# RWKV attention with routed experts: the experts' activations transposed by DMA in 16-bit halves, and their down products a step later

## The chip, the cores and the metric

The kernel runs on one core of a Trainium2 chip. The metric is the device time of one execution in microseconds (us). TensorE (PE, with its weight loads as PEld) multiplies matrices into PSUM, VectorE (DVE), ScalarE (ACT) and GpSimd (POOL) work on elements, SyncE (SP) issues most DMAs; GpSimd issues the gathers, the scatters and the accumulating DMAs. Each engine has one queue and works through it in order; a DMA that is issued runs by itself.

## The reference

On 2048 tokens of 512 channels, all in float32, with `xn = layernorm(x)`:

```
r, v, k = split(xn @ W_rvk.T)                      # attention branch
y = sigmoid(r) * wkv(time_decay, time_first, k, v) # a recurrence over 8 x 256 = 2048 tokens
                                                   # (the input is 1 x 2048 x 512)
attn = y @ W_out.T

probs = softmax(xn @ classifier_w.T)               # 12 choices: 8 experts, 4 without weights
idx = top_k(probs + bias, 2); rw = probs[idx] * 1.5
expert_e = (silu(xn @ gate_e.T) * (xn @ up_e.T)) @ down_e.T     # inner size 256
ffn = sum_e w_e * expert_e + xn * (weight of the 4 without weights)

out = x + attn + ffn
```

## The kernel before

**The beginning.** `x` is normalised, stored as `xs` in DRAM, and transposed into `xnT`; the router finds for each token its two experts, and lays out 25 tiles of 128 places, each of one expert (`token_i`: which token stands at a place, `to_i`: which row of `out` it is added to, `wplace`: with which weight). `out` is filled with `x` by DMA (`begin_output`). Every later part is added to `out` by accumulating DMAs, except for the last block of 512 tokens, which is read back (`read_out`), added up on VectorE and written. The accumulating DMAs on `out` follow one another, each waiting for the earlier one that may touch the same rows; a scatter may touch all of them.

**The middle** is a list of work written out by hand: `table` holds entries with a due time and is sorted by it. The due times are no times of the machine; they set the order only, and each engine's queue has the instructions in that order. There are three kinds:

- `project(b, c)` for block `b` and channel group `c`: three groups of matmuls (`pk`, `pv`, `pr`), each of four matmuls of 128x512 (eight records, since each is done in two passes), evicted from PSUM by ScalarE. Two PSUM banks (`ps_mm`) serve them in turn. Eight entries of `attention` (output products `pw`, four matmuls each) take places among them (`after`).
- `scan(*unit)`: the recurrence of one block and channel group in four stages: scan 0 (VectorE), exponentials (ScalarE), two scans and five elementwise operations (VectorE), reciprocal and product `yT` (VectorE). Scan 0 is 2.7 us, the third stage about 5.3, the last about 4.
- `step(i, n)`: one step of the experts' pipeline over the 25 tiles. A tile is gathered (`gather`, GpSimd), packed into 16-bit halves by ScalarE and transposed by a DMA of SyncE (`flip`: `xp`, then `xq`), united to float32 by ScalarE (`unite`: `xgT`), multiplied with the expert's gate and up weights (`up`: `pg`, four matmuls), put through `silu(g) * u` (`activate`: `th` on ScalarE and VectorE, `act` on VectorE), transposed by TensorE through PSUM (`turn_act`: two transposes into `pa`, and `actT` by ScalarE), multiplied with the down weights (`finish`: `po`, two matmuls of 128x512), weighted (`yo`, ScalarE) and scatter-added to `out` (GpSimd). In step `i` the gate and up products of tile `i` are made, with the transposes of tile `i - 1`'s activations in their middle and its down products behind them. Weights are loaded two steps ahead (`fetch`, `fetch_down`), with three buffers each.

**The end.** After the table come the last tile's transposes, the output products of block 2 (`last_rows`, with the last tile's down products after the first of them), a conditional loop for more than 25 tiles which is not entered, and block 3: reading back, its output products, the last sums and the writing of them. The order of that last part, after `manual.close()`, is no longer set by hand.

Pools give the number of buffers: `ex_p` two of each tag, `wk1` one, `gathered` two, `rows` three, `ewp` three.

Of the kernel before, what the change touches and what calls it, by code (L numbers as in the profile page):

```python
# [26 lines left out]
F32 = mybir.dt.float32  # L27
BF16 = mybir.dt.bfloat16
I32 = mybir.dt.int32
U16 = mybir.dt.uint16  # L30
# [5 lines left out]
P = 128  # L36
T = 2048
C = 512
# [7 lines left out]
INTER = 256  # L46
IC = INTER // P
# [4 lines left out]
TILES = 25  # L52
# [7 lines left out]
def layer(ctx: ExitStack, tc: tile.TileContext, x, w_rvk, w_out, decay, first, cls, ebias, gu, down, out):  # L60
    nc = tc.nc

    def pool(name, bufs, **kw):
        return ctx.enter_context(tc.tile_pool(name=name, bufs=bufs, **kw))
# [6 lines left out]
    wk1 = pool("wk1", 1)  # L71
# [6 lines left out]
    ex_p = pool("exp", 2)  # L78
# [180 lines left out]
    def project(b, c):  # L259

        n = f"{b}_{c}"
        for name, m in (("k", 2), ("v", 1), ("r", 0)):
            ps = ps_mm.tile([P, TB], F32, tag="mm", name=f"p{name}{n}")
            for k in range(CC):
                nc.tensor.matmul(  # L265
                    ps,
                    wrvk_sb[m][:, k, c * P : (c + 1) * P],
                    xnT[b][:, k, :],
                    start=(k == 0),
                    stop=(k == CC - 1),  # L270
                )
                if k < CC - 1:
                    yield
            t = kvp.tile([P, TB], F32, tag=name, name=f"{name}{n}")
            if name == "r":
                nc.scalar.activation(t, ps, AF.Exp, scale=-1.0)
            else:
                nc.scalar.copy(t, ps)
            kvr[b, c, name] = t
            yield  # L280
# [270 lines left out]
    st = {}  # L551

    def gather(i, token=token_i):

        xg = gathered.tile([P, C], F32, tag="xg", name=f"xg{i}")
        nc.gpsimd.indirect_dma_start(  # L556
            out=xg,
            out_offset=None,
            in_=xs,
            in_offset=bass.IndirectOffsetOnAxis(ap=token[:, i : i + 1], axis=0),  # L560
        )
        st[i] = {"xg": xg}

    def fetch(i, which=which_i):

        e = nc.values_load(
            which[0:1, i : i + 1],
            engines=(SP,),
            min_val=0,
            max_val=E - 1,  # L570
            skip_runtime_bounds_check_because="a sum of E - 1 comparisons",
        )
        w = ewp.tile([P, CC, 2 * INTER], F32, tag="gw", name=f"gw{i}")
        nc.sync.dma_start(w, gu[bass.ds(e, 1)].rearrange("o p c n -> p (o c) n"))
        st[i].update(w=w, e=e)

    def fetch_down(i):
        d = ewp.tile([P, IC, C], F32, tag="dw", name=f"dw{i}")
        nc.sync.dma_start(d, down[bass.ds(st[i]["e"], 1)].rearrange("o p c n -> p (o c) n"))
        st[i]["d"] = d  # L580
# [9 lines left out]

    def flip(i):

        xp = ex_p.tile([P, 2, C], U16, tag="xp", name=f"xp{i}")
        nc.scalar.copy(xp, st[i]["xg"].bitcast(U16).rearrange("p (c h) -> p h c", h=2))  # L594
        xq = ex_p.tile([P, 2 * CC, P], U16, tag="xq", name=f"xq{i}")
        nc.sync.dma_start_transpose(xq, xp.rearrange("p h c -> p (h c)"))
        st[i]["xq"] = xq

    def unite(i):

        xgT = ex_p.tile([P, CC, P], F32, tag="xgT", name=f"xgT{i}")
        nc.scalar.copy(  # L602
            xgT.bitcast(U16).rearrange("p c (t h) -> p c t h", h=2),
            st[i]["xq"].rearrange("p (h c) t -> p c t h", h=2),
        )
        st[i]["xgT"] = xgT

    def up(i, cs):

        if 0 in cs:  # L610
            st[i]["pg"] = ps_gu.tile([P, 2, INTER], F32, tag="gu", name=f"pg{i}")
        pg = st[i]["pg"]
        for c in cs:
            nc.tensor.matmul(  # L614
                pg, st[i]["xgT"][:, c, :], st[i]["w"][:, c, :], start=(c == 0), stop=(c == CC - 1)
            )

    def activate(i):
        pg = st[i]["pg"]

        th = ex_p.tile([P, INTER], F32, tag="th", name=f"th{i}")
        nc.scalar.activation(th, pg[:, 0, :], AF.Tanh, scale=0.5)  # L622
        nc.vector.scalar_tensor_tensor(th, th, 1.0, pg[:, 0, :], ALU.add, ALU.mult)  # L623
        act = ex_p.tile([P, INTER], F32, tag="act", name=f"act{i}")
        nc.vector.tensor_mul(act, th, pg[:, 1, :])
        st[i]["act"] = act

    def turn_act(i):
        pt = ps_tr.tile([P, IC, P], F32, tag="tr", name=f"pa{i}")
        for c in range(IC):  # L630
            nc.tensor.transpose(pt[:, c, :], st[i]["act"][:, c * P : (c + 1) * P], ident)  # L631
        actT = ex_p.tile([P, IC, P], F32, tag="actT", name=f"actT{i}")
        nc.scalar.copy(actT, pt)  # L633
        st[i]["actT"] = actT

    def finish(i, weight=wplace, to=to_i):
        po = ps_o.tile([P, C], F32, tag="o", name=f"po{i}")
        for c in range(IC):
            nc.tensor.matmul(  # L639
                po, st[i]["actT"][:, c, :], st[i]["d"][:, c, :], start=(c == 0), stop=(c == IC - 1)  # L640
            )
        yo = rows.tile([P, C], F32, tag="rb", name=f"yo{i}")
        nc.scalar.activation(yo, po, AF.Identity, scale=weight[:, i : i + 1])  # L643
        nc.gpsimd.indirect_dma_start(  # L644
            out=out,
            out_offset=bass.IndirectOffsetOnAxis(ap=to[:, i : i + 1], axis=0),
            in_=yo,
            in_offset=None,
            compute_op=ALU.add,
        )  # L650
        del st[i]

    def step(i, n):

        if i + 2 < n:
            fetch(i + 2)
        if i < n:
            up(i, (0, 1))
        if i > 0:
            turn_act(i - 1)  # L660
        if i < n:
            up(i, (2, 3))
            activate(i)
        if i + 3 < n:
            gather(i + 3)
        if i > 0:
            finish(i - 1)
        if i + 2 < n:
            flip(i + 2)
            fetch_down(i + 2)  # L670
        if i + 1 < n:
            unite(i + 1)

# [61 lines left out]
    fill(4)  # L735
    next(stages[0])
    flip(0)
    flip(1)
    fill(4)
    next(stages[0])  # L740
# [5 lines left out]

    UNIT = 20.0
    ahead = [p for p in [project(*u) for u in units[LEAD:]] for _ in range(3)]  # L750
    after = {14: (0, 0), 17: (0, 1), 20: (0, 2), 23: (0, 3), 34: (1, 0), 37: (1, 1), 40: (1, 2), 43: (1, 3)}
    groups = len(ahead) + len(after)
    total = groups * 3.43 + TILES * 5.5
    table = []
    for u in range(1, len(units)):
        for k, at in enumerate((0, 4, 6, 12)):
            table.append(((u - 1) * UNIT + at, 1, stages[u]))
    for m in range(groups):
# [7 lines left out]
    for i in range(TILES):  # L766
        table.append((6 + total * i / TILES, 1, iter([(step, i, TILES)])))
# [9 lines left out]
    last_rows = attention(NTB - 2)  # L777
    next(last_rows)
    finish(TILES - 1)
    read_xn(NTB - 1)  # L780
    whole(last_rows)
# [9 lines left out]
    with tc.If(count > TILES):  # L791
        with tc.For_i(TILES, MAX_TILES, 1) as i:
            cols = {}
            for name, a, dt in (
                ("which", which_i, I32), ("token", token_i, I32), ("to", to_i, I32), ("weight", wplace, F32)
            ):
                cols[name] = small.tile([P, 1], dt, tag=f"col_{name}", name=f"col_{name}")
                nc.vector.tensor_copy(cols[name], a[:, bass.ds(i, 1)])
            gather(0, cols["token"])
            fetch(0, cols["which"])  # L800
            fetch_down(0)
            turn(0)
            up(0, range(CC))
            activate(0)
            turn_act(0)
            finish(0, cols["weight"], cols["to"])
# [46 lines left out]
```

## Time and profile before

| what | value |
|---|---|
| median of 3 runs | 397.49 us (396.98 to 397.56) |
| the profiled execution | 398.03 us |
| its span | 396.2 us |
| DMA, mean | 216 GB/s, 85.78 MB |
| DMA transposes `xq` | 25, issue 1.25 us each on SyncE, landing 2.8 / 4.8 / 5.1 us (min / median / max) |
| scatters to `out` | 25, landing 4.9 / 5.6 / 10.1 us |
| rows added to `out` (L722) | 12, landing 4.0 / 5.3 / 6.7 us |
| `xp` copy, `xgT` copy, `actT` copy (ScalarE) | 1.04, 1.16, 0.37 us |
| SyncE's waits before `xq` | 212.4 us in 24 waits, for ScalarE |

The profile lists instructions by line of the kernel, engine and operation with the names of the tiles (`pg<-gw,xgT` writes `pg` from `gw` and `xgT`). Times are in us from the span's start. In the order of time, a line gives start, duration, engine, line, operation, and in brackets how long the engine was idle before it and what ended that. A matmul's end is modelled: of consecutive matmuls, the distance of their starts says what one costs.

### The profile page before, as it was taken

How to read it: one execution, taken by the hardware profiler on the slowest of the kernel's cores; microseconds unless marked ns; L12 is line 12 of the kernel's file. 1: busy time of each engine (PE TensorE's matmuls, PEld its weight loads, DVE VectorE, ACT ScalarE, POOL GpSimd, SP SyncE). 2: the span in 40 equal slices, each digit the busy share in tenths (PEclk: the TensorE clock that was granted, in tenths of full speed). 3: DMA queues.
4: the chain of work that ended last, by engine and by line, in shares of the span. 5: the costliest groups of instructions: out<-in, count | busy, mean ns of one | idle time of the engine just before them, and what ended most of it. 6: DMA issues, size and time to landing. Idle time of an engine off the chain costs nothing. (4 is left out here: it accounts for less than half of the span.)

```text
span 396.2 us, 3539 instructions
## 1 busy us (share of the span) xinstructions
PE 379.4 (96%) x1040; PEld 173.8 (44%) x1040; DVE 271.1 (68%) x397; ACT 154.0 (39%) x255; POOL 98.5 (25%) x130
## 2 busy tenths in 40 slices
PE   0999999999999999999999999999999999999996
PEld 0555445444444444444444444444444444444442
DVE  4872998997673919766659395569395784883905
ACT  2765111553444453344354443354444253432000
POOL 4002001420232414133333232222142331122220
PEclk9999999999999999999999999999999999999999
DMA  7998907645765855879778899765857979664593
GB/s 270 409 393 315 318 28 321 142 148 185 240 191 145 261 158 201 256 230 282 215 170 226 239 242 257 220 187 141 282 191 231 266 220 278 151 119 91 124 169 149
DMA packets 50372, 85.78 MB, mean 216 GB/s; under 512 B 29680, under 2 KB 29808, under 8 KB 46576
## 3 DMA queue, kind: packets, MB, share of 16 engines
q1 hardware_dynamic: 42816, 64.84, 48.0%
q0 software_dynamic: 7536, 20.71, 25.2%
q8 instruction: 8, 0.13, 0.1%
q14 instruction: 12, 0.10, 0.1%
HBM read 63.78 MB, written 19.40 MB: 210 GB/s over the span
## 5 line engine op out<-in xcount | busy, mean ns | idle before, releaser
L614 PE MATMUL pg<-gw,xgT 128*128 128x512 f32 x200 | 93.9, 592 | 0.0
L644 POOL DMA_INDIRECT out_dram<-yo,to_i x25 | 42.4, 1697 | 147.3 <-ACT yo L643 116.6
L265 PE MATMUL pk<-xnT,wrvk 128*128 128x512 f32 x128 | 58.8, 596 | 0.0
L265 PE MATMUL pr<-xnT,wrvk 128*128 128x512 f32 x128 | 57.7, 592 | 0.0
L265 PE MATMUL pv<-xnT,wrvk 128*128 128x512 f32 x128 | 57.6, 593 | 0.0
L707 PE MATMUL pw<-wout_sb,yT 128*128 128x512 f32 x128 | 56.8, 593 | 0.1
L323 DVE RECIPROCAL den<-den 128x512 f32<-128x512 f32 x16 | 53.5, 3345 | 0.0
L614 PEld LDWEIGHTS pg<-gw,xgT 128*128 128x128 f32 x200 | 36.1, 190 | 36.3 <-issue 34.9
L639 PE MATMUL po<-dw,actT 128*128 128x512 f32 x100 | 47.1, 593 | 0.5 <-ACT actT L633 0.5
L309 DVE TENSOR_TENSOR_SCAN sums<-obv,state,a 128x512 f32<-128x512 f32 x16 | 20.5, 1283 | 35.0 <-ACT obv L303 35.0
L623 DVE SCALAR_TENSOR_TENSOR th<-th,pg 128x256 f32<-128x256 f32 x25 | 10.5, 419 | 41.8 <-ACT th L622 41.7
L556 POOL DMA_INDIRECT xg<-xs,token_i x25 | 29.8, 1193 | 33.1 <-DVE empty L543 27.5
L707 PEld LDWEIGHTS pw<-wout_sb,yT 128*128 128x128 f32 x128 | 24.2, 190 | 30.6 <-issue 30.6
L265 PEld LDWEIGHTS pk<-xnT,wrvk 128*128 128x128 f32 x128 | 23.8, 190 | 31.2 <-issue 31.2
L265 PEld LDWEIGHTS pr<-xnT,wrvk 128*128 128x128 f32 x128 | 24.2, 190 | 30.1 <-issue 30.1
L265 PEld LDWEIGHTS pv<-xnT,wrvk 128*128 128x128 f32 x128 | 24.2, 190 | 30.1 <-issue 29.9
L643 ACT ACTIVATE yo<-po,wplace 128x512 f32<-128x512 f32 x25 | 17.2, 687 | 35.9 <-PE po L639 35.9
L639 PEld LDWEIGHTS po<-dw,actT 128*128 128x128 f32 x100 | 18.9, 190 | 24.7 <-issue 23.4
L602 ACT COPY xgT<-xq 128x1024 uint16<-128x1024 uint16 x25 | 29.0, 1160 | 0.0
L594 ACT COPY xp<-xg 128x1024 uint16<-128x1024 uint16 x25 | 25.8, 1037 | 0.0
L633 ACT COPY actT<-pa 128x256 f32<-128x256 f32 x25 | 9.3, 371 | 37.8 <-PE pa L631 37.8
L230 PE MATMUL pt<-ident,x 128*128 128x128 f32 x64 | 12.6, 326 | 11.8 <-DVE x L220 10.1
(149 smaller groups left out, 360.3 us busy)
## 6 DMA issues: line engine op xcount, KB each, us to landing
gw<-in_gu_dram SPq DMA_DIRECT2D x25, 1024.0 KB, 6.9
dw<-in_down_dram SPq DMA_DIRECT2D x25, 512.0 KB, 5.3
x<-in_x_dram SPq DMA_DIRECT2D x16, 256.0 KB, 5.3
xs<-x SPq DMA_DIRECT2D x16, 256.0 KB, 4.7
wrvk<-in_w_rvk_dram SPq DMA_DIRECT2D x3, 1024.0 KB, 7.3
xrow<-xs SPq DMA_DIRECT2D x12, 256.0 KB, 5.7
out_dram<-xrow POOLq DMA_DIRECT2D x12, 256.0 KB, 5.3
wout_sb<-in_w_out_dram SPq DMA_DIRECT2D x1, 1024.0 KB, 9.5
```

The costliest lines, as they stand in the source:

```text
L230: nc.tensor.transpose(pt[:, j * P : (j + 1) * P], xt[b * NJ + j][:, c * P : (c + 1) * P], ident)
L265: nc.tensor.matmul(ps, wrvk_sb[m][:, k, c * P : (c + 1) * P], xnT[b][:, k, :], start=(k == 0), stop=(k == CC - 1),)
L309: nc.vector.tensor_tensor_scan(sq, bs, a2, s[:, 3:4], ALU.add, ALU.mult)
L323: nc.vector.reciprocal(den, den)
L556: nc.gpsimd.indirect_dma_start(out=xg, out_offset=None, in_=xs, in_offset=bass.IndirectOffsetOnAxis(ap=token[:, i : i + 1], axis=0),)
L594: nc.scalar.copy(xp, st[i]["xg"].bitcast(U16).rearrange("p (c h) -> p h c", h=2))
L602: nc.scalar.copy(xgT.bitcast(U16).rearrange("p c (t h) -> p c t h", h=2), st[i]["xq"].rearrange("p (h c) t -> p c t h", h=2),)
L614: nc.tensor.matmul(pg, st[i]["xgT"][:, c, :], st[i]["w"][:, c, :], start=(c == 0), stop=(c == CC - 1))
L639: nc.tensor.matmul(po, st[i]["actT"][:, c, :], st[i]["d"][:, c, :], start=(c == 0), stop=(c == IC - 1))
L643: nc.scalar.activation(yo, po, AF.Identity, scale=weight[:, i : i + 1])
L644: nc.gpsimd.indirect_dma_start(out=out, out_offset=bass.IndirectOffsetOnAxis(ap=to[:, i : i + 1], axis=0), in_=yo, in_offset=None, compute ...
L707: nc.tensor.matmul(po, yT[b][:, c, j * P : (j + 1) * P], wout_sb[:, c, :], start=(c == 0), stop=(c == CC - 1),)
```

## The change

The activations of 23 of the 25 tiles go through ScalarE and a DMA transpose, as the gathered tokens do: `flip_act` packs `act` into halves (`ap`) and SyncE transposes them (`aq`), and `unite_act` makes `actT` of them one step later. The down products of tile `i - 2` are made in step `i` where those of `i - 1` were. The last two tiles keep the transposes on TensorE, and the last step has two tiles' down products. The down weights are fetched one step later. `xp` gets one buffer in place of two. The due times are set a little closer (19.4 for 20.0 a unit of the scan, 280.92 for 288.42 in all).

```diff
     def flip(i):
 
-        xp = ex_p.tile([P, 2, C], U16, tag="xp", name=f"xp{i}")
+        xp = wk1.tile([P, 2, C], U16, tag="xp", name=f"xp{i}")
...
+    def flip_act(i):
+
+        ap = wk1.tile([P, 2, INTER], U16, tag="ap", name=f"ap{i}")
+        nc.scalar.copy(ap, st[i]["act"].bitcast(U16).rearrange("p (c h) -> p h c", h=2))
+        aq = wk1.tile([P, 2 * IC, P], U16, tag="aq", name=f"aq{i}")
+        nc.sync.dma_start_transpose(aq, ap.rearrange("p h c -> p (h c)"))
+        st[i]["aq"] = aq
+
+    def unite_act(i):
+        actT = ex_p.tile([P, IC, P], F32, tag="actT", name=f"actT{i}")
+        nc.scalar.copy(
+            actT.bitcast(U16).rearrange("p c (t h) -> p c t h", h=2),
+            st[i]["aq"].rearrange("p (h c) t -> p c t h", h=2),
+        )
         st[i]["actT"] = actT
...
         if i + 2 < n:
             fetch(i + 2)
-        if i < n:
-            up(i, (0, 1))
-        if i > 0:
+        if i > 1:
+            unite_act(i - 2)
+        if 0 < i < n - 1:
+            flip_act(i - 1)
+        up(i, (0, 1))
+        if i == n - 1:
             turn_act(i - 1)
-        if i < n:
-            up(i, (2, 3))
-            activate(i)
+        up(i, (2, 3))
+        activate(i)
         if i + 3 < n:
             gather(i + 3)
-        if i > 0:
+        if i > 1:
+            finish(i - 2)
+        if i == n - 1:
             finish(i - 1)
         if i + 2 < n:
             flip(i + 2)
-            fetch_down(i + 2)
+        if 2 <= i + 1 < n:
+            fetch_down(i + 1)
         if i + 1 < n:
             unite(i + 1)
...
-    UNIT = 20.0
+    UNIT = 19.4
...
-    total = groups * 3.43 + TILES * 5.5
+    total = groups * 3.43 + TILES * 5.2
```

More of the change, by code (lines that the diff above doesn't have):

```diff
@@ L634, in turn_act @@
         st[i]["actT"] = actT
+    def flip_act(i):
[10 more added lines that the diff above has]
+        )
+        st[i]["actT"] = actT
     def finish(i, weight=wplace, to=to_i):
```

## The prediction

> **What bounds the kernel now.** I read four views, in this order: the page, the table by stage, the order of time in one expert step, and the order of time at the end.
>
> ```profile
> PE 379.4 (96%) x1040; PEld 173.8 (44%) x1040; DVE 271.1 (68%) x397; ACT 154.0 (39%) x255; POOL 98.5 (25%) x130
> PEclk9999999999999999999999999999999999999999
> ```
>
> TensorE is busy for 96% of the span at the full clock. The table by stage says where the other 4% lies (columns: stretch, length, busy time of each engine, clock, DMA share, GB/s):
>
> ```profile
> 110.00:140.00 30.00, 29.55 (x73) 12.99 (x72) 19.27 (x22) 13.33 (x22) 10.49 (x8) 1.00 0.72 214
> 170.00:200.00 30.00, 30.00 (x75) 13.43 (x74) 21.24 (x24) 11.36 (x20) 10.73 (x10) 1.00 0.92 257
> 370.00:396.20 26.20, 22.19 (x52) 9.32 (x50) 11.62 (x14) 0.00 (x0) 5.15 (x5) 1.00 0.59 130
> ```
>
> In the expert steps TensorE never stops, except for 0.45 us in one of them (step 4: its down products waited for `actT`, behind a state copy on ScalarE that waited for VectorE). Any TensorE instruction taken out there shortens the stretch. The order of time in step 9 gives the price of one tile's transposes and ScalarE's room:
>
> ```profile
> 180.32 3.60 PE L265 MATMUL pk<-xnT,wrvk 128*128 128x512 f32 x8
> 183.75 1.88 PE L614 MATMUL pg<-gw,xgT 128*128 128x512 f32 x4
> 183.95 0.58 ACT L278 COPY k<-pk 128x512 f32<-128x512 f32 x1 [1.80 <-PE pk L265]
> 185.47 0.38 PE L631 MATMUL pa<-ident,act 128*128 128x128 f32 x2
> 185.68 1.88 PE L614 MATMUL pg<-gw,xgT 128*128 128x512 f32 x4
> 185.94 0.37 ACT L633 COPY actT<-pa 128x256 f32<-128x256 f32 x1 [1.41 <-PE pa L631]
> 187.40 1.88 PE L639 MATMUL po<-dw,actT 128*128 128x512 f32 x4
> 187.60 0.38 ACT L622 ACTIVATE th<-pg 128x256 f32<-128x256 f32 x1 [1.29 <-PE pg L614]
> ```
>
> Eight matmuls of 512 columns take 183.75 - 180.32 = 3.43 us. The same eight with the two transposes between take 187.40 - 183.75 = 3.65 us. So a pair costs 0.22 us, and not the 0.38 of its row, which overlaps its neighbours.
>
> The end is another matter. GpSimd's rows there:
>
> ```profile
> 358.26 0.92 POOL L722 DMA_DIRECT2D out_dram<-xrow  x1 [5.07 <-DVE xrow L719]
> 363.55 1.61 POOL L644 DMA_INDIRECT out_dram<-yo,to_i  x1 [4.37 <-ACT yo L643]
> 370.15 1.56 POOL L644 DMA_INDIRECT out_dram<-yo,to_i  x1 [5.00 <-DMA out_dram<-yo,to_i]
> 375.59 2.73 POOL L722 DMA_DIRECT2D out_dram<-xrow  x3 [3.88 <-DVE xrow L719]
> 379.30 0.86 POOL L722 DMA_DIRECT2D out_dram<-xrow  x1 [0.97 <-DVE xrow L719]
> ```
>
> The adds into `out` go one after another: the last scatter (370.15) waited for the one before it to land, and the rows at 375.59 for the last scatter (the first of those rows was ready on VectorE at 374.21, over a microsecond earlier). Then the reading back of the last block starts at 382.29, VectorE gets it at 386.23, and its last add starts at 392.38, when TensorE is done. There this chain is only 1.50 us ahead of TensorE.
>
> **What the change removes.** 23 of the 25 pairs of transposes (the last two tiles keep theirs): 23 x 0.22 = 5.1 us of TensorE on the path. The down products come a step later with `actT` long ready, so step 4's 0.45 us goes too: 5.5 us. The profiled run took 398.03 us with a span of 396.2; the sum is made on the span and taken off the median 397.49, 0.54 us under that run.
>
> **What it adds, and what hides it.** ScalarE: the packing of 512 halves (new). The rows nearest are 1.04 us for 1024 halves and 0.58 to 0.63 us for 512 elements: 0.52 to 0.63. The uniting: half of 1.16, or 0.63. Less the 0.37 us of `actT`, this is 0.7 to 0.9 us a tile, about 18 us in 154. It stands ahead of `th`, where ScalarE is empty from 184.53 to 187.60 less 0.37, or 2.7 us, in most steps (1.6 in two, none in step 4). If that cover is gone, `th` is late by up to 1.3 us, and TensorE notices only if an eviction of `pk`, `pv` or `pr` behind it comes after both banks are full. I take 0.
>
> ScalarE's new waits: packing waits for VectorE's `act`. Behind it on ScalarE stand `th`, `yo` and the evictions. In all 24 steps `act` was ready 2.9 to 8.9 us before ScalarE came there; 0. Uniting waits for a transfer issued a step earlier. Steps start 12.2 us apart, a few 8.8; from the issue to the next uniting 7.4 us is left in a short step. The transfer's landing isn't shown; the `xq` transfer of twice the size lands in 2.8 to 5.1 us, and a lower bound is the 1.25 us that SyncE spends on issuing one. I take the upper end, as it queues behind the 1 MB of `gw`; 0. The skill's page "DMA: Bandwidth & Descriptors" (section "Anatomy of one DMA") has about 2.0 us plus bytes over 436 GB/s for a GpSimd transfer; for 128 KB that is an estimate of 2.3 us, and the sum would be the same.
>
> SyncE: each step issues one more transpose (1.25 us), ahead of `xq` and `dw`. It spent 212 us waiting at `xq` for ScalarE; 0. DMA: 23 x 128 KB is 3 MB more on 85.8; shares reach 0.92 in some stages, yet loads have two steps of lead; 0.
>
> A rule speaks against all this. "VectorE: DVE Perf Modes" (section "Rules for kernel authors") sends a 128x128 transpose to TensorE wherever PSUM will do as its goal. By that rule nothing is won and the time stays at 397.49. The stage's row says otherwise of this kernel: there TensorE has no idle time, and ScalarE and SyncE have.
>
> `xp` with one buffer: in the steps its last reader lands a step earlier; 0. In the beginning flips 0 and 1 follow each other, and the second copy must wait for the first transfer: issued at 73.15, landed 2.8 to 5.1 us later, then 1.05 us of copy and 0.58 of evicting `v`: 77.6 to 79.9. TensorE needs that bank at 78.26. I take 2.8, since DMA is idle before 75 (share 0.21): no stall; the other end is 1.6 us.
>
> `dw` is fetched one step later for products two steps later: its lead grows from one step to two. In step 23 SyncE now has this load and a transpose ahead of the last rows' loads, which ran from 341.75 to 362.47 and are needed by VectorE after 366; 0. Timetable: sorted by its new due times (total 280.9 for 288.4, units 19.4 for 20.0), the order stays but for nine pairs of neighbours. Three put ScalarE's exponentials ahead of work it would have done first (two evictions, the last step); there ScalarE may wait for VectorE's 2.7 us of scan 0, which is due 4 us before; 0. The last scan ends earlier, so VectorE's rows at the end wait for TensorE alone.
>
> **What the change moves to the end.** Step 24 now has two down products. TensorE comes to them 5.5 us earlier plus the 1.72 us of the product that step 1 no longer has: 7.2 us. So scatter 22 takes the place of 363.55 at 356.3. Scatter 23 is ready 1.7 us later but must wait for 22 to land; scatter 24 for 23; the rows for 24. Before, only one such wait stood between there and the rows. Its price, issue to next issue: 6.60 (363.55 to 370.15), 5.44 (370.15 to 375.59), in the steps 6.1 to 7.3 where a row waited for a scatter. I take 6.6 (loads beside it, as before), 6.2 (middle of the rows), 5.4: 356.3 + 18.2 = 374.5, only 1.1 us before 375.59. Four rows at 0.91 (2.73 / 3): 378.2, against 380.16 before (379.30 + 0.86). Reading back starts 2.13 us on (380.16 to 382.29), VectorE 3.94 on (to 386.23), at 384.3. Its eight operations (386.23 to 390.88, and one of 0.69) take 5.3: 389.6, against 393.07. So the end comes 3.5 us earlier, and TensorE, ending at 386.9, waits for it. 397.49 - 3.5 = **394.0 us**. Bounds: three gaps of 5.44 give the full 5.5; three of 7.33 give 378.3 for the first row, and an end at 393.3, 0.2 us later than now.
>
> **Rivals.** *The full gain*: the chain at the end keeps up and TensorE's 5.5 us arrive whole, 392.0 us. For it: the two last gaps were short, with few loads beside. Against: all three gaps must be as short as the shortest that the trace has, 5.44 us.
>
> *Slower through the scatters at the end*: the same three gaps, longer. From 7.24 us each on, nothing is left; at 8.0 the end is 2.3 us later, 399.8 us. For it: one landing took 10.1 us. Against: the median is 5.6 and load falls in the end.
>
> *ScalarE waits after all*: for the transfer, or in the beginning (1.6 us); half of the gain goes: 397.49 - 1.75 = 395.7 us, within the range.
>
> *It does not do what it says*: if weight loads rather than matmuls set the pace, the pair would not cost 0.22; the 3.65 against 3.43 excludes it.
>
> **How the numbers follow.** Chain at the end as worked out: 0.60; full gain 0.14; ScalarE or the beginning 0.12; scatters at the end at no gain or slower 0.14. A measurement of this kernel tells about 0.2%, 0.8 us, from no change. Faster: 0.60, 0.14 and 0.08 of the third, 0.82; same: 0.04 of the third and 0.03 of the last, 0.07; slower: the rest of the last, 0.11. The range reaches from the full gain, 392.0, to 396.6, which leaves out the worst gaps.
>
> **What would show it.** Two `pa` groups in place of 25, TensorE busy about 5 us less and still full in the steps; scatters of the end about 6 us apart with DMA as releaser; VectorE's last adds waiting for the reading back and not for `pw`. Wrong, if TensorE shows gaps in the steps with `xgT` or evictions as releaser, or if its last product again ends last.

## The result, and the profile after

The changed kernel takes 399.72 us (median of four runs, 398.75 to 399.91), the kernel before beside it 397.34 us: 1.0056 of the time before, interval 1.0038 to 1.0074. It is 0.6% slower, where 394.0 us had been predicted. Runs more than 1.5% above the fastest of their kernel are left out of medians and ratios; this concerns three of twelve runs of one version below, with the rows of block 1 earlier. The profiled execution took 399.70 us with a span of 397.9 us, 1.67 us more than the one of before.

The page first, its lines of busy time and of the clock:

```profile
PE 374.3 (94%) x994; PEld 169.8 (43%) x994; DVE 270.6 (68%) x397; ACT 170.7 (43%) x278; POOL 99.0 (25%) x130
PEclk9999999999999999999999999999999999999997
```

TensorE has 5.1 us less to do (379.4 before), ScalarE 16.7 us more. The last digit of the clock is 7 where TensorE idles at the end. The table by stage (stretch, length, busy time of each engine, clock, DMA share, GB/s):

```profile
110.00:140.00 30.00, 29.02 (x68) 12.65 (x67) 17.27 (x22) 14.00 (x25) 8.96 (x8) 1.00 0.87 240
170.00:200.00 30.00, 30.00 (x71) 13.27 (x70) 21.28 (x25) 14.26 (x24) 10.66 (x9) 1.00 1.05 267
370.00:397.90 27.90, 17.80 (x41) 7.33 (x39) 6.62 (x10) 0.00 (x0) 5.16 (x5) 0.92 0.59 132
```

The steps are still full, but the stretch from 110 us now lacks 0.98 us of TensorE where it had lacked 0.45. In the last stretch TensorE works 17.8 of 27.9 us: it no longer sets the end. One step in order of time shows the new pipeline at work:

```profile
180.95 3.60 PE L614 MATMUL pg<-gw,xgT 128*128 128x512 f32 x8
181.82 0.68 ACT L646 COPY actT<-aq 128x512 uint16<-128x512 uint16 x1
182.40 0.62 ACT L639 COPY ap<-act 128x512 uint16<-128x512 uint16 x1
184.39 1.88 PE L655 MATMUL po<-dw,actT 128*128 128x512 f32 x4
184.59 0.38 ACT L622 ACTIVATE th<-pg 128x256 f32<-128x256 f32 x1 [1.57 <-PE pg L614]
```

The eight gate/up matmuls take 184.39 - 180.95 = 3.44 us, with no transposes in their middle (3.65 before). The two copies stand in ScalarE's idle time, and `th` still waits for TensorE. So the mechanism works where it was meant to. GpSimd's rows at the end show what took the gain:

```profile
353.88 0.92 POOL L743 DMA_DIRECT2D out_dram<-xrow  x1 [4.88 <-issue]
358.90 1.67 POOL L660 DMA_INDIRECT out_dram<-yo,to_i  x1 [4.10 <-ACT yo L659]
368.39 1.56 POOL L660 DMA_INDIRECT out_dram<-yo,to_i  x1 [7.83 <-issue]
374.12 1.55 POOL L660 DMA_INDIRECT out_dram<-yo,to_i  x1 [4.17 <-issue]
379.44 3.61 POOL L743 DMA_DIRECT2D out_dram<-xrow  x4 [3.77 <-DMA out_dram<-yo,to_i]
```

Three scatters (22, 23 and 24) in a row, and then the four rows at once. All of them were ready before: scatter 22's `yo` at 357.16, scatter 23's at 358.88, the first row's sum on VectorE at 365.83, the last one's at 374.61. The rows begin at 379.44, where those of before began at 375.59. The chain of waits now ends in this list and no longer in TensorE:

```profile
354.72 3.45 PE po L655 x8
358.90 24.65 DMA out_dram<-yo,to_i
383.68 5.17 DMA orows<-out_dram
```

And VectorE waits for the reading back, not for `pw`. Its last add before the change (L716), and its last rows after it:

```profile
392.38 0.69 DVE L716 TENSOR_TENSOR orows<-orows,pw 128x512 f32<-128x512 f32 x1 [1.50 <-PE pw L707]
```

```profile
388.87 2.08 DVE L715 SCALAR_TENSOR_TENSOR orows<-xrows,zw,orows 128x512 f32<-128x512 f32 x3 [14.26 <-DMA orows<-out_dram]
392.12 1.87 DVE L737 TENSOR_TENSOR orows<-orows,pw 128x512 f32<-128x512 f32 x3
```

TensorE's end moved from 392.35 to 387.95 us, 4.4 us earlier; VectorE's last add ends at 394.0, 0.9 us later than before.

**Where the list becomes full.** All 37 adds into `out` (25 scatters and 12 rows) follow one another. In the kernel before, the last eight intervals between them, from the row at 324.17 to the first of the last rows at 375.59, had room left: four of the adds (339.44, 351.57, 358.26 and 363.55) were issued within 0.7 us of their source. In the changed kernel the same stretch runs from the row at 319.68 to 379.44 and has nine intervals, since the lag (the down products two steps behind, for one) leaves one tile more to be added there. Every one of these adds came 1.7 us or more after its source, once the one before had landed: 59.76 / 9 = 6.64 us each. The lag brings one add of 6.6 us more to an end that had about 1.5 us of room, and TensorE's 4.4 us do not cover it.

### The profile page after: what moved, and what is told of

It reads as the page before. It is cut to its first block, busy times and chain, and to the rows that moved or that the text cites. A ratio compares the mean times of both kernels' runs of the same rounds, so it can differ in the third digit from the quotient of the medians.

```text
span 397.9 us, 3507 instructions
## 1 busy us (share of the span) xinstructions
PE 374.3 (94%) x994; PEld 169.8 (43%) x994; DVE 270.6 (68%) x397; ACT 170.7 (43%) x278; POOL 99.0 (25%) x130
## 4 chain that ended last, share of the span: by engine, by line
PE 76%; DMA 9%; DVE 7%; ACT 4%; issue 2%; DVEq 0%; SPq 0%; ACTq 0%
PE pg L614 21%; PE pr L265 12%; PE pk L265 12%; PE pv L265 11%; PE po L655 10%; PE pw L728 7%; DMA out_dram<-yo,to_i 6%; PE pt L230 2%; DMA orows<-out_dram 1%; DMA x<-in_x_dram 1%; ACT x L222 1%; DVE tok L512 1%; PE pi L520 1%; ACT xnT L231 0%; DVE orows L715 0%
## 5 line engine op out<-in xcount | busy, mean ns | idle before, releaser
L614 PE MATMUL pg<-gw,xgT 128*128 128x512 f32 x200 | 90.1, 592 | 0.0
L614 PEld LDWEIGHTS pg<-gw,xgT 128*128 128x128 f32 x200 | 37.9, 190 | 47.4 <-issue 46.2
L556 POOL DMA_INDIRECT xg<-xs,token_i x25 | 30.6, 1224 | 42.9 <-DVE empty L543 27.5
L309 DVE TENSOR_TENSOR_SCAN sums<-obv,state,a 128x512 f32<-128x512 f32 x16 | 20.5, 1282 | 25.3 <-ACT obv L303 25.3
L655 PEld LDWEIGHTS po<-dw,actT 128*128 128x128 f32 x100 | 18.9, 190 | 25.2 <-issue 23.2
L622 ACT ACTIVATE th<-pg 128x256 f32<-128x256 f32 x25 | 9.6, 383 | 42.8 <-PE pg L614 42.8
## 6 DMA issues: line engine op xcount, KB each, us to landing
wout_sb<-in_w_out_dram SPq DMA_DIRECT2D x1, 1024.0 KB, 10.1
```

The costliest lines, as they stand in the source:

```text
L309: nc.vector.tensor_tensor_scan(sq, bs, a2, s[:, 3:4], ALU.add, ALU.mult)
L556: nc.gpsimd.indirect_dma_start(out=xg, out_offset=None, in_=xs, in_offset=bass.IndirectOffsetOnAxis(ap=token[:, i : i + 1], axis=0),)
L614: nc.tensor.matmul(pg, st[i]["xgT"][:, c, :], st[i]["w"][:, c, :], start=(c == 0), stop=(c == CC - 1))
L655: nc.tensor.matmul(po, st[i]["actT"][:, c, :], st[i]["d"][:, c, :], start=(c == 0), stop=(c == IC - 1))
```

## The experiments

Theory A: the two scatters of the last step, one add more in a serial list, decide the time; TensorE's gain is real. Against it stood: the DMA transposes themselves (their packets beside the scatters) make the landings long; the place of five loads that start there does; the denser timetable does. In each paragraph the ratio is to the kernel before on the same chip.

**Control.** The changed kernel again, beside three of the runs below (catching up in step 17, the loads, the old timetable). The others ran at other times, some on another chip; the kernel before took 397.66 to 397.77 us beside all of them.

> The changed kernel again, beside the next ones: 399 to 400 us by every theory.

398.76 us (12 runs, 396.86 to 400.88), 1.0027, interval 1.0008 to 1.0045. A kernel whose end is this list scatters by 4 us from run to run here; the kernel before stayed within 2.0 us in the 29 runs beside it (396.63 to 398.62). Differences below 1 us between two kernels of the first sort mean little. Its profile has the first of the last rows at 376.96 and a span of 396.1.

**One add fewer at the end.** Tile 22's scatter goes to another tensor in DRAM.

```diff
+    aside = dram.tile([T + P, C], F32, tag="aside", name="aside")
...
-            out=out,
+            out=aside if i == TILES - 3 else out,
```

> The changed kernel, but tile 22's scatter goes to another DRAM tensor (its share is left out of the output), so that nothing that adds into out follows it any more. Theory A (the chain of adds into out at the end sets the time, and the second scatter of the last step is a link too many): scatter 23 goes out near 359 in place of 368.4, the four rows near 372 in place of 379.4, and TensorE ends last again; 393 to 394.5 us. Rival B (every DMA has become slower through the 23 more transposes, and the one link is of little account): 397 to 399. Rival C (the loss lies in the steps, not at the end): 399.7, unchanged.

394.08 us, 0.9920, interval 0.9905 to 0.9935. GpSimd's rows at the end:

```profile
356.53 1.87 POOL L661 DMA_INDIRECT aside<-yo,to_i  x1 [3.35 <-DMA out_dram<-xrow]
358.70 1.62 POOL L661 DMA_INDIRECT out_dram<-yo,to_i  x1 [0.30 <-issue]
367.50 1.55 POOL L661 DMA_INDIRECT out_dram<-yo,to_i  x1 [7.17 <-issue]
372.90 3.62 POOL L744 DMA_DIRECT2D out_dram<-xrow  x4 [3.85 <-DMA out_dram<-yo,to_i]
```

Scatter 23 takes the place that scatter 22 had. The rows come 6.5 us earlier than at 379.44, and 4.1 us earlier than the control's; the median falls by 4.7 us against the control. All of the new DMA load is still there. One serial add fewer turns a loss of 0.3 to 0.6% into a gain of 0.8%.

**The lag alone.** The kernel before with the down products two steps behind, TensorE's transposes and the old due times.

```diff
-        if i > 0:
+        if i > 1:
+            finish(i - 2)
+        if i == n - 1:
             finish(i - 1)
...
-            fetch_down(i + 2)
+        if 2 <= i + 1 < n:
+            fetch_down(i + 1)
```

> The kernel before with one part of the change: down products two steps behind and down weights fetched a step later, with TensorE's transposes kept and the old due times. Theory A: TensorE's work is that of before, but the last step's two scatters put one gap of some 6 us into the chain at the end; about 1 us slower than before, 398 to 399 us. Rival B (the transposes by DMA are what slows): no change, 397.3.

400.61 us, 1.0069, interval 1.0056 to 1.0082: more than was expected of it, and slower than the whole change. Its end:

```profile
360.79 1.61 POOL L644 DMA_INDIRECT out_dram<-yo,to_i  x1 [4.19 <-ACT yo L643]
369.50 1.56 POOL L644 DMA_INDIRECT out_dram<-yo,to_i  x1 [7.11 <-issue]
375.05 1.55 POOL L644 DMA_INDIRECT out_dram<-yo,to_i  x1 [3.99 <-issue]
380.48 3.62 POOL L723 DMA_DIRECT2D out_dram<-xrow  x4 [3.88 <-DMA out_dram<-yo,to_i]
```

Not one activation is transposed by DMA here, and the three intervals are 8.71 + 5.55 + 5.43 = 19.7 us, as in the control (8.61 + 5.66 + 5.22 = 19.5). The first row is 4.9 us later than before; less the 1.5 us that the list was ahead of TensorE, this is 3.4 us, and the span grew by 3.5 (399.7 for 396.2). Up to there this list had room: scatters 20, 21 and 22 and the row at 355.68 came within 0.5 us of their sources. So the last step's additional scatter makes the loss without a list that is full from 319 us on. The lag costs about 3 us by itself; the transposes by DMA then win part of it back through an earlier start (358.90 or 357.47 for 360.79).

**Catching up earlier.** The lag of two ends in step 17, which makes two tiles' down products; from there on TensorE transposes and the products follow one step behind. The last step then has one tile's products, as before.

```diff
-        if i > 1:
+        if 1 < i <= 17:
             unite_act(i - 2)
-        if 0 < i < n - 1:
+        if 0 < i < 17:
             flip_act(i - 1)
...
-        if i == n - 1:
+        if i >= 17:
             turn_act(i - 1)
...
-        if i > 1:
+        if 1 < i <= 17:
             finish(i - 2)
-        if i == n - 1:
+        if i >= 17:
             finish(i - 1)
```

> The changed kernel up to step 17, which makes two tiles' down products; from there on transposes on TensorE and down products one step behind, as in the kernel before. 17 pairs of transposes are gone: 17 x 0.22 = 3.7 us of TensorE, less the 0.5 us that step 4 now loses. Theory A (the extra link in the chain of the end takes the gain): in the steps around 17 the chain has pauses of several us and swallows the extra scatter, the end is that of the kernel before, and TensorE ends last; 394 to 395 us. Rival B (all DMAs slower through the added transposes): the chain is still full at the end, 397 to 399.

394.55 us (394.00 to 394.62), 0.9914, interval 0.9902 to 0.9927, faster than the kernel before and than the changed one. GpSimd's rows at the end, and the chain that ended last:

```profile
360.12 1.87 POOL L660 DMA_INDIRECT out_dram<-yo,to_i  x1 [4.37 <-ACT actT L633]
368.23 1.56 POOL L660 DMA_INDIRECT out_dram<-yo,to_i  x1 [6.24 <-DMA out_dram<-yo,to_i]
373.60 3.62 POOL L743 DMA_DIRECT2D out_dram<-xrow  x4 [3.80 <-issue]
```

```profile
379.23 9.69 PE pw L728 x22
388.95 0.69 DVE orows L737
```

The additional scatter (tile 16's) was issued 4.2 us late at 281.89, and the next, at 290.13, on time: in the middle the list has room and takes it. At the end TensorE is last again. With 16 pairs removed (the expectation had counted 17), 16 x 0.22 = 3.5 us less the 0.53 us that the stall of step 4 grew by give 3.0; measured 397.68 - 394.55 = 3.1.

**The same, with the uniting earlier.** In step 4 TensorE waits for `actT`. In the changed kernel, ScalarE's rows there and TensorE's wait:

```profile
126.81 0.19 ACT L322 COPY state<-sums 128x2 f32<-128x2 f32 x1 [2.79 <-DVE sums L311]
126.91 0.67 ACT L646 COPY actT<-aq 128x512 uint16<-128x512 uint16 x1
...
127.63 1.98 PE L655 MATMUL po<-dw,actT 128*128 128x512 f32 x4 [0.98 <-ACT actT L646]
```

The uniting stands behind the state copy, which waits for VectorE. Moved to the end of the step before:

```diff
-        if 1 < i <= 17:
-            unite_act(i - 2)
...
         if i + 1 < n:
             unite(i + 1)
+        if 0 < i < 17:
+            unite_act(i - 1)
```

> As the kernel that catches up in step 17, but the uniting of the activations stands at the end of the step in which they were packed, behind the uniting of the next tokens, and not at the beginning of the next step. Theory: the 0.98 us in which TensorE waits in step 4 come from the place of actT behind the state copy on ScalarE; earlier, actT is ready before, TensorE is full from 110 to 140 us (30.00 of 30.00), and since TensorE ends last here, the time is 1 us less than 394.55: about 393.6, 0.990 of the kernel before. Rival: ScalarE now waits in each step for the transfer that was issued in the same step, 5 us in the median, and the yo copy, the evictions of pk, pv and pr and the packing behind it come late: TensorE shows gaps in the steps, the time is 395 or more.

393.55 us (393.06 to 393.73), 0.9893, interval 0.9878 to 0.9908: the fastest version here. By stage, and ScalarE's waits (in total, times, longest):

```profile
110.00:140.00 30.00, 30.00 (x71) 13.30 (x70) 17.68 (x24) 13.81 (x26) 8.39 (x7) 1.00 0.95 245
```

```profile
ACT actT L646 <- DMA aq<-ap: 10.5, 4, 3.6
```

The stall is gone and the time is 1.0 us less, as expected. The rival's wait is there too, 10.5 us in four steps, and no matmul was late for it.

**Catching up in step 22.** As the one in step 17, with the last condition at 22:

```diff
-        if i == n - 1:
+        if i >= 22:
             finish(i - 1)
```

> The changed kernel, but step 22 makes two tiles' down products, and from there on TensorE transposes and the lag is one step; so the last step has one scatter fewer than in the changed kernel, and the additional scatter is issued near 345 us, inside the stretch in which each add into out waited for the one before in the changed kernel (from 319 us on). Theory that counts the whole full stretch: the number of adds from 319 us to the end is the same, only the place of one differs; the chain stays full, the first of the last rows comes at 377 to 379 us, the time 397 to 399.5 us. Theory that counts only the last step: with three adds in place of four behind the last step's products the end has the slack of the kernel before, the first rows come near 374 us and TensorE ends last: 394 to 395 us.

396.36 us, 0.9967, interval 0.9954 to 0.9979: neither theory's time. The list was full from the row at 319.36 on, as the first theory had it, with each add there late by 1.4 us or more, and the first of the last rows came at 375.78, 1.2 us ahead of the control's. The nine intervals took 6.27 us each (56.42 / 9; control 57.33 / 9 = 6.37). The two profiled executions differ by as much, 1.13 us (396.82 and 397.95); the medians differ by 2.4 us because the one profile lies 0.5 us above its median and the other 0.8 us below. A catch-up inside the full stretch thus gives back about half of what one in step 17 does (2.4 us of 4.2 by the medians).

**The loads beside the first scatter of the end.** In the changed kernel scatter 22 takes 8.4 us to land (358.90 to 367.31). The row's landing that releases it also releases five loads of 256 KB on SyncE, issued from 358.20; these are the suspected reason. Here four of the five stand ahead of the row's own and are issued from 344.04.

```diff
+    read_xn(NTB - 1)
...
-    read_xn(NTB - 1)
```

> The changed kernel with the loads of block 3's rows ahead of those of block 2's in SyncE's queue. In the changed kernel the landing of row (1,3) lets go scatter 22 and five loads of 256 KB at the same moment, and the scatter lands after 8.4 us. Theory A2 (those loads make the first gap of the end long): the four loads of block 3 run before, scatter 22 lands after some 6 us, the gap to scatter 23 falls from 9.5 to about 7; 397 to 398 us. Rival (the gap has another reason): unchanged, 399.7.

398.21 us, 1.0010, interval 0.9998 to 1.0022. The interval after scatter 22 fell to 6.09 us (8.61 in the control), but scatter 21 now took 8.8 us to land (346.49 to 355.28), and scatter 22 started 3.0 us later (360.51). So the loads lengthen the scatters beside them here, and moving them only changed the place of the cost. They don't explain the whole length: in the kernel before the same five loads stood beside scatter 23, and it landed in 5.9 us (363.55 to 369.40). There two of the five were issued 1.3 and 1.8 us behind the scatter (364.86 and 365.33), in the changed kernel all of them by 359.99, 1.1 us behind it. Whether that makes the difference was not tested.

**The rows of block 1 earlier.** The sums of block 1 take earlier places in the table, to empty the list ahead of the end.

```diff
-    after = {14: (0, 0), 17: (0, 1), 20: (0, 2), 23: (0, 3), 34: (1, 0), 37: (1, 1), 40: (1, 2), 43: (1, 3)}
+    after = {14: (0, 0), 17: (0, 1), 20: (0, 2), 23: (0, 3), 26: (1, 0), 29: (1, 1), 32: (1, 2), 35: (1, 3)}
```

> The changed kernel with the four rows of block 1 eight places earlier in the list (26, 29, 32, 35 for 34, 37, 40, 43), where scatters did not follow one another closely. Theory A in its wider form (the chain runs full from 319 us on, so that scatter 22 already starts 1.7 us after it is ready): scatters 19 to 22 wait for nothing, scatter 22 goes out near 357.5, the chain at the end still has its extra link; 395 to 397 us. Theory A in its narrow form (only the last three gaps count): 399 or more. Rival C: unchanged, 399.7.

398.83 us (395.81 to 399.90 in nine runs), 1.0013, interval 0.9992 to 1.0033, no gain that can be told. The list was jammed earlier (scatter 16, at 302.63, came 13.9 us after its source) and TensorE had 207.47 busy us in 210 from 140 us on. Scatter 22 was on time (359.85, its `yo` at 359.57), but TensorE had lost 2.5 us on the way, and the first of the last rows came at 378.31. So this run doesn't separate the theories.

**Do the transposes make the landings long?** The scatter's median landing rose from 5.6 to 6.5 us. In the trace the packets of an `xq` transfer (256 bytes each) take 25 ns on average, by the median over the 25 tiles, for 17.9 before. The first tile's take 21.1 for 17.9, when no activation has been transposed; so `xp`'s new place was suspected. First, `xp`, `ap` and `aq` aligned to 64 bytes by two small tiles put ahead of them:

```diff
+    odd = pool("odd", 1)
...
+    pad = wk1.tile([P, 8], F32, tag="pad", name="pad")
...
+    pad2 = odd.tile([P, 8], F32, tag="pad2", name="pad2")
```

> The changed kernel with 32 bytes of padding ahead of the one-buffer pool, and 32 behind it: xp, ap and aq now begin at multiples of 64 bytes in each partition, where in the changed kernel they begin 32 beyond one (before, xp began at a multiple of 512). Theory D (the transposes' packets are slow because of where xp and ap begin, and slow down the scatters beside them): the transpose of xq takes 1.1 us of packets again in place of 1.4, lone scatters land 5.5 us after their issue in place of 6.3, and the full chain of the last 60 us gets shorter; 395 to 398 us. Rival B (the added transposes are the cause): packets and landings as in the changed kernel, 399.7.

398.08 us, 1.0015, interval 1.0001 to 1.0030; packets of 23.2 ns by the same measure (control 22.5) and scatters landing in 6.6 us (control 6.6): alignment isn't it. Then the kernel before with `xp` in `wk1`:

```diff
-        xp = ex_p.tile([P, 2, C], U16, tag="xp", name=f"xp{i}")
+        xp = wk1.tile([P, 2, C], U16, tag="xp", name=f"xp{i}")
```

> The kernel before, but xp has one buffer in the pool of one buffer, as in the changed kernel; the lag, the transposes on TensorE and the timetable are those of before. Theory that the additional DMA load comes from the 23 added transposes and from the bunched scatters: landings as in the kernel before (scatter 5.6, xq 4.8 us in the median), the time 397.5 us (396.9 to 398). Rival that xp's new place makes the transposes of the tokens slower for all: xq 5.2 us or more, scatters 6 us or more in the median with no other change, the time at most 0.5 us more since TensorE covers it. In the beginning the second packing waits some 3 us for the first transfer, without a stall of TensorE.

397.82 us, 1.0004, interval 0.9994 to 1.0013. Scatters land in 6.4 us, `xq` in 5.1, a packet takes 27.6 ns on average: most of the rival's landings, without one transpose added, and the time doesn't change. Last, the changed kernel with `xp` in a pool of its own (one buffer) at the upper end of SBUF:

```diff
+    xpp = pool("xpp", 1)
...
-        xp = wk1.tile([P, 2, C], U16, tag="xp", name=f"xp{i}")
+        xp = xpp.tile([P, 2, C], U16, tag="xp", name=f"xp{i}")
```

> The changed kernel, but xp stands in a pool of its own, with one buffer, at the upper end of SBUF beside the other experts' tiles, where the kernel before has it, and no longer in the pool wk1 at the lower addresses; nothing else differs. The kernel before with xp in wk1 alone had scatters of 6.4 us and xq of 5.1 us in the median, for 5.6 and 4.8. Theory that xp's place lengthens the landings and that these longer landings make the chain at the end late: scatters 6.0 us or less in the median, first of the last rows 376 us or earlier, time 395 to 397 us. Rival that the two down products of the last step make it late by themselves (as in the kernel with the lag alone, 400.6 us, whose xp stood in the old place): the time stays at 398 to 400 us whatever the landings are. Should the landings not fall either, one buffer or the added transposes lengthen them, and not the place.

398.19 us, 1.0010, interval 0.9993 to 1.0027. DMA issues with their median landing:

```profile
xq<-xp SPq DMA_TRANSPOSE x25, 4.2
out_dram<-yo,to_i POOLq DMA_INDIRECT x25, 6.1
```

The packets of `xq` are back at 17.9 ns, so for the packets it is the place and not the single buffer. `xq` lands in 4.2 us (5.4 and 4.6 in the two profiles of the changed kernel, but 4.3 in the aligned version, whose packets are slow), the scatters in 6.1 (6.5 and 6.6). But the first row comes at 376.67, as in the control, and the time stays: a real effect on the packets, not shown for the landing of `xq`, and not the cause of the loss.

**The old timetable.** The changed kernel with the due times of before.

```diff
-    UNIT = 19.4
+    UNIT = 20.0
...
-    total = groups * 3.43 + TILES * 5.2
+    total = groups * 3.43 + TILES * 5.5
```

> The changed kernel with the old due times (20.0 and 5.5). Theory A: the order of the list has little to do with it; 399 to 400.5 us, scatters 22 to 24 again one behind the other. Rival E (the nine pairs that trade places cost the time): 397.5 or less.

397.89 us (396.44 to 401.50), 1.0014, interval 0.9993 to 1.0035; the end has the same shape (scatters at 356.72, 364.88, 370.38, rows at 375.76). Not to be told from the control.

## Why the prediction was wrong

**What held.** The removed transposes: 5.1 us of TensorE, by the sum and by the profile (379.4 to 374.3). ScalarE's copies at 0.62 and 0.68 us, hidden; `th` still waits for `pg`. The uniting waited for a transfer once, 0.2 us, `aq` landing in 5.0 us at the median, where 5.1 had been taken; the reason given, that it queues behind `gw`, was not tested. From the Trainium skill's page "DMA: Bandwidth & Descriptors" (section "Anatomy of one DMA") the prediction had an estimate of 2.3 us, by a figure for transfers issued by GpSimd. This transpose, issued by SyncE among other transfers, took over twice that; the measurement decides. `xp` with one buffer made ScalarE wait 3.4 us once, in the beginning, without a stall of TensorE. SyncE and the timetable: nothing seen. The rule of the Trainium skill's page "VectorE: DVE Perf Modes" (section "Rules for kernel authors"), a 128x128 transpose to TensorE where PSUM will do, was not borne out here: with 16 pairs moved off TensorE and the uniting earlier, the time is 0.9893 of the one before. The loss of the whole change came from the lag.

**Step 4.** The 0.45 us were to vanish; they became 0.98. The prediction saw that `actT` had stood behind the state copy and took it to be "long ready" one step later. But its uniting stands in ScalarE's queue at the same place, behind the state copy, and takes 0.67 us where the copy of `actT` took 0.36; TensorE also came there 2.4 us earlier, the state copy only 2.2. TensorE's lead was therefore 4.4 us and not 5.5. Moving the uniting removed the stall.

**The end, which decides.** The forecast named the right list, worked with the right three intervals, and had "slower through the scatters at the end" as a rival at 0.14. What failed is the sum for the end, in two of its terms:

- *The start, 356.3 us.* Measured 358.90. Of these 2.6 us, 1.1 is TensorE's smaller lead, and 1.5 a wait: the list was already full when scatter 22 came, behind the row at 353.88. The step counted the waits from scatter 22 on only; the profile of before had shown adds late by 4 to 5 us at 331 and 347, and one more add in that stretch was not carried through. In the control scatter 22 waited hardly at all (357.47, 0.4 us behind its `yo`), so this wait differs from execution to execution.
- *Three gaps, 18.2 us.* Measured 9.50 + 5.73 + 5.32 = 20.5 (control 19.5, lag alone 19.7). The last two were over-priced by 0.5 to 0.7 us; the first, at 6.6, was short by 2 to 3 us in all three executions. It was taken from the 6.60 of before, with the same five loads beside it; here, where the loads come closer together, the scatter took 7.5 to 8.4 us to land. When four of them were moved ahead, this interval fell to 6.09. Why the same loads cost more than before stays open. The rival was put down because "load falls in the end". As a mean it does (DMA share 0.50 from 350 to 370 us), but not beside this scatter (0.72 from 358.90 to 367.31); and beside scatter 23 of before, which landed sooner, it was 0.94, so the share doesn't tell a scatter's length here.

The first of the last rows was thus 4.9 us later than 374.5. Behind it, reading back began 0.6 us after the rows for 2.13 taken (-1.5), landed in 5.2 us for 3.94 (+1.2), and the tail behind VectorE's last add took 3.9 us for 3.1 (+0.8). Together about 5.3 us, and the profiled span is 1.7 us longer instead of 3.5 us shorter. The gaps alone would have left 1.2 us of the 3.5. In the control the first row came 2.5 us later than 374.5, 1.2 by the start and 1.3 by the gaps. So the mechanism was the forecast one, a chain at the end that keeps TensorE's gain from arriving; its price was too low.

**The chances.** The case of no gain or a loss got 0.14, though its bounds stood in the sum itself: three gaps of 7.24 us were the point of no gain, and one landing of 10.1 us was in the trace. The three gaps measured 6.85 us on average, and the start was 2.6 us later. The range was cut at 396.6 by leaving out just these "worst gaps"; a list that had been late by 4 to 5 us twice before the end deserved the larger chance.

## What to carry to other kernels

Where accumulating DMAs into one tensor wait for one another, count them as an engine of its own: how many adds are left from the point where the list is last empty, times the measured interval (6.3 to 6.6 us here). A deeper pipeline makes up its lag at its end. Here it could be made up in the middle at no cost that shows, where the list has room; with the uniting earlier as well the change becomes a gain of 1.1% (0.9893). Before a load is called low at some place, look at what the same landing releases.

## What the runs showed of the hardware

- At the end of the changed kernel a scatter of 256 KB landed in 8.4 us with five loads of the same size released with it (358.90 to 367.31), the next, without them, in 5.0 us (368.39 to 373.38). With four of the five loads moved ahead, the first took 5.0 us, and the scatter that now stood beside them 8.8. In the kernel before, a scatter beside the same five loads, more spread out, took 5.9.
- The place of a tile in SBUF changed a DMA transpose: the packets of an `xq` transfer took 17.9 ns on average (median over the tiles) from a pool beside the experts' tiles and 22.5 to 25 ns from `wk1` in the otherwise same kernel. A single packet took 18 ns in the median in both; the mean rises by some slow ones. One buffer or two and the alignment to 64 bytes were excluded; what it is about the place stays open.
- The time of the changed kernel scatters by 4.0 us in 12 runs (396.86 to 400.88), that of the version with the rows earlier by 4.1 us in nine, that of the catch-up in step 17, which TensorE ends, by 0.6 us in five.
